# Second layer of a gated cross-attention network: transposed weights of both query tiles side by side, one product of 224 columns per head pair

## The chip, the cores and the metric

The kernel runs on one NeuronCore of a Trainium2 chip. The metric is the device time of one execution in microseconds; the median of three runs of the kernel before is 2099.33 us (2097.63 to 2100.96). All data are fp32 unless a line says otherwise. The engines are called PE (TensorE, the matmuls), VectorE (DVE), ScalarE (ACT), GpSimd (POOL) and SyncE (SP, which issues the DMAs); each of them takes its instructions in the order in which the program writes them for it.

## The reference

Eight batch elements, each with 224 tokens of 512 features and a context of 750 tokens of 512 features, go through two layers. A layer is a gated cross-attention and then a gated feed-forward network (FFN), each on the layer-normed input, each added back with a gate tanh(g):

```python
x = x + jnp.tanh(g_xattn[0]) * _L0_xattn_ref(_layernorm(x), ctx, ctx, ...)   # 16 heads of 32
x = x + jnp.tanh(g_ffn[0])   * _L0_ffn_ref(_layernorm(x), ...)               # ternary weights, conv, silu
x = x + jnp.tanh(g_xattn[1]) * _L1_xattn_ref(_layernorm(x), ctx, mask, ...)  # 8 heads of 64, masked
x = x + jnp.tanh(g_ffn[1])   * _L1_ffn_ref(_layernorm(x), ...)               # FP4-quantized weights and inputs
```

The change lies in the second layer's attention, of which this is the core:

```python
attn = jnp.einsum('bhnd,bhmd->bhnm', q, k) * SCALE      # 8 heads, 224 queries, 750 keys
attn = jnp.where(mask[:, None, :, :], attn, -jnp.inf)
attn = jax.nn.softmax(attn, axis=-1)
out = jnp.einsum('bhnm,bhmd->bhnd', attn, v)
```

## The kernel before

The main loop runs over n = 0 to 15: n = 0 to 7 are the batch elements in the first layer's attention (`attention16`), n = 8 to 15 the same elements in the second layer's (`attention8`). The text calls n = 8 "element 8" and so on. The last FFN of all elements follows in a stage of its own.

In `attention8` the 224 queries are cut into NT = 2 tiles of TP = 112, the 750 keys into NKT = 6 pieces of CP = 125, the eight heads into KC = 4 pairs g. One element is eight slots; slot = 2g + i is head pair g and query tile i, so even slots have i = 0 and odd slots i = 1. A slot does this:

1. PE: scores of both heads (L757, four matmuls of 375 columns, the two heads on the upper and lower 64 rows of the array), into two PSUM tiles `ps_half` of two banks each. There are two such tiles in all.
2. PE: the product of the values with the weights of the slot before (L720): 6 pieces x 2 heads, 112 columns each, heads side by side in the array's columns, summed in the bank `ps_pa`.
3. VectorE: mask and row maximum of each head (L774), its negative (L786).
4. ScalarE: exp with the row sum, one per head (L795), into the SBUF tile `room`.
5. PE: six transposes for each head (L817), from `room` back into a `ps_half` tile; a head's transposes need its exp.
6. ScalarE: the copy of each head's transposed weights into `room` as `pT` (L822), from where the next slot's product reads them. The next slot's scores need the same PSUM tiles, so they need these copies.

`weights_room` gives `p` and `pT` one of three stretches of `room` in turn. When both tiles of two head pairs are through, `divided` splits the reciprocal row sums (L731, L458, L462), transposes them (L468, copied by ScalarE as `sT`, L470), spreads them over the rows (L738, copied as `inv`, L742) and multiplies the product bank by them (L746). The last product and the second `divided` of an element run inside the next element (`rest`).

The order of the work around this is written by a planner with nominal costs. Other work stands in queues of generators whose pieces carry nominal PE and VectorE microseconds: the values and keys of this and the next element (L383, L325, copied by ScalarE, L392 and L334), the queries (L200, L354; L201, L363), the output projection (L429, L440), and `beside`, which holds the last part of the first FFN (L961, L1040, L1075) and the FP4 quantization and transposition of the last FFN's weights (`fp4_steps` L1115 to L1130, transposes L1156, copies L1174 and L1184). `fill(us, queue)` takes pieces until `us` of nominal PE time are used; `pace(us, beside)` takes pieces until VectorE has `us` of nominal work since the maxima. `finish` empties a queue. A slot fills 0.8 and 1.0 ahead of the two exps, 1.2 ahead of the transposes and 1.7 behind them (3.0 in the last element); `finish(values)` in slot 1 makes sure that the values are there for the first product. One pace call (1.5) stands ahead of the exps, one (3.5) behind them. Whatever copy a piece needs is written into ScalarE's order at the same place.

PSUM beside that: two banks `ps_m`, one `ps_t`, one `ps_pa`.

Of the kernel before, what the change touches and what calls it, by code (L numbers as in the profile page):

```python
# [36 lines left out]
B, S, D = 8, 224, 512  # L37
M = 750
TP = 112
# [3 lines left out]
KC = D // 128  # L43
MH = M // 2
WIDE = 500
CP = 125
NKT = M // CP
# [19 lines left out]
class Net:  # L67
# [125 lines left out]
    def transposed(self, dst, src, i, bank="t"):  # L193

        nc = self.nc
        half = src.dtype == BF16
        pt = self.ps(bank, [128, KC, TP], BF16 if half else F32)
        ident = self.ident16 if half else self.ident
        for k in range(KC):
            nc.tensor.transpose(pt[:, k, :], src[:, k * 128 : (k + 1) * 128], ident[:TP, :TP])  # L200
        nc.scalar.copy(dst[:, :, i * TP : (i + 1) * TP], pt)  # L201
# [499 lines left out]
    def attention8(self, n, soon, values, queue, beside, ends):  # L701

        nc, pool, job = self.nc, self.att, self.jobs[n]
        kT, qT = job["kT"], job["qT"]
        rows = [slice(h * 64, (h + 1) * 64) for h in range(2)]
        masks = self.masks(job["raw"])  # L710
        total = pool.tile([TP, NT, 2, KC], F32, name="total")
        banks = {}

        def product(g, i, pT):
            if g % 2 == 0 and i == 0:
                banks["pa"] = self.ps("pa", [128, 2, S])
            for j in range(NKT):
                for h, r in enumerate(rows):
                    col = g * 128 + h * 64
                    nc.tensor.matmul(  # L720
                        banks["pa"][r, g % 2, i * TP : (i + 1) * TP],
                        lhsT=job["v"][j][:, col : col + 64],
                        rhs=pT[:, h, j * TP : (j + 1) * TP],
                        start=j == 0,
                        stop=j == NKT - 1,
                    )

        def divided(pair):

            inv = pool.tile([TP, NT, 2, 2], F32, name="invs", bufs=2)  # L730
            nc.vector.reciprocal(inv, total[:, :, :, 2 * pair : 2 * pair + 2])  # L731
            transposed = self.stat_rows(self.stat[1][pair], inv)
            yield 0, 1.3
            sT = transposed("m")
            yield 0.1, 0.3
            pi = self.ps("t", [128, 2, S])
            for k in range(2):
                nc.tensor.matmul(  # L738
                    pi[:, k, :], lhsT=self.spread_r[:, k, :], rhs=sT, start=True, stop=True
                )  # L740
            across = pool.tile([128, 2, S], F32, name="inv")
            nc.scalar.copy(across, pi)  # L742
            yield 0.4, 0.6
            if pair == 0:
                job["aT"] = pool.tile([128, KC, S], F32, name="aT")
            nc.vector.tensor_tensor(  # L746
                job["aT"][:, 2 * pair : 2 * pair + 2, :], banks["pa"], across, ALU.mult
            )
            yield 0, 0.6

        before = None
        for slot in range(KC * NT):
            g, i = divmod(slot, NT)
            sc = [self.ps("half", [TP, 2, 512]) for _ in rows]
            for c in range(2):
                for h, r in enumerate(rows):
                    nc.tensor.matmul(  # L757
                        sc[h][:, c, :MH],
                        lhsT=qT[r, g, i * TP : (i + 1) * TP],
                        rhs=kT[g][r, c * MH : (c + 1) * MH],  # L760
                        start=True,
                        stop=True,
                    )
            if slot == 0:
                next(ends, None)
            elif slot == 1:
                self.finish(values)
            if slot:
                product(*before)
            nms = []  # L770
            for h in range(2):
                src = sc[h][:, :, :MH]
                mx = self.small.tile([TP, 1], F32, name="mx")
                nc.vector.tensor_tensor_reduce(  # L774
                    out=src,
                    in0=src,
                    in1=masks[i],
                    scale=1.0,
                    scalar=-MASKED,
                    op0=ALU.add,  # L780
                    op1=ALU.max,
                    accum_out=mx,
                )

                nms.append(self.small.tile([TP, 1], F32, name="nm"))
                nc.vector.tensor_scalar(nms[h], mx, -1.0e38, -1.0, ALU.max, ALU.mult)  # L786
            self.behind = 0
            if slot == 4:
                next(first)
            if not soon and (n + 1 < 2 * B or slot < 3):  # L790
                self.pace(1.5, beside)
            p = self.weights_room(TP, M, 2)
            for h, us in enumerate((0.8, 1.0)):
                self.fill(us, queue)
                nc.scalar.activation(  # L795
                    p[:, h, :].rearrange("p (c k) -> p c k", c=2),
                    sc[h][:, :, :MH],
                    AF.Exp,
                    bias=nms[h],
                    accum_out=total[:, i, h, g : g + 1],  # L800
                )
            if not soon:
                self.pace(3.5 if n + 1 < 2 * B or slot < 2 else 2.5, beside)
            self.fill(1.2, queue)
            if slot == 3:
                first = divided(0)
                next(first)
            if slot == 4:
                next(first)
            if slot == 4:  # L810
                next(first)
            pT = self.weights_room(CP, NKT * TP, 2)
            for h in range(2):
                pt = self.ps("half", [CP, 2, 512])
                half = NKT // 2
                for j in range(NKT):
                    nc.tensor.transpose(  # L817
                        pt[:, j // half, j % half * TP : (j % half + 1) * TP],
                        p[:, h, j * CP : (j + 1) * CP],
                        self.ident[:TP, :TP],  # L820
                    )
                nc.scalar.copy(  # L822
                    pT[:, h, :].rearrange("p (c k) -> p c k", c=2), pt[:, :, : half * TP]
                )
            before = g, i, pT
            self.finish(soon)
            self.fill(1.7 if n < 2 * B - 1 else 3.0, queue)
        if n < 2 * B - 1:
            self.finish(queue)
        second = divided(1)  # L830
        next(second)

        def rest():
            product(*before)
            yield 1.3, 0
            yield next(second)
            yield next(second)
            yield next(second)

        return rest()  # L840


# [771 lines left out]
```

## Time and profile before

| | us |
|---|---|
| median of 3 runs | 2099.33 |
| the profiled execution | 2097.81 |
| its span | 2096.0 |
| second layer's stretch, 1049 to 1718 | 669.00, PE busy 663.07 |
| VectorE, ScalarE, GpSimd busy in that stretch | 433.39, 301.72, 60.60 |
| L720, the product: 1536 records there | 87.72 busy |
| L817, the transposes: 768 records there | 94.05 busy |

A timeline row gives the start in the span, the length, the engine, the line, what is written and read, and how many records are merged in it. An fp32 matmul leaves two records, its two passes, a transpose leaves one: the program issues 12 matmuls L720 in each of 64 products, and the trace has 1536 records. A row of PE ends later than the next begins, as matmuls are pipelined, so the cost of a run on PE is read from its start to the next run's start. "PEld" are weight loads, which mostly lie beside a running matmul. A bracket at the end of a row is the engine's idle time ahead of it and what ended it. In a row of stretches the first number after the stretch is its length, then come each engine's busy time, the granted clock, the DMA share and GB/s.

### The profile page before, as it was taken

The page shows a single profiled execution, that of the slowest core. Times are in us where ns is not written, and L with a number is a line of the kernel's source. Part 1 is how long each engine was busy: PE and PEld are TensorE (multiplying, and loading weights), DVE is VectorE, ACT ScalarE, POOL GpSimd, SP SyncE. Part 2 cuts the span into 40 slices and gives each one's busy share as a digit, 9 for nine tenths or more (in the row PEclk, how much of TensorE's full clock was granted, in tenths as well). Part 3 has the DMA queues.
Part 4 walks back from the last instruction along what each step waited for, and adds up shares of the span by engine and source line. Part 5 has one row for each costly group of instructions (what it writes and reads, how often), then busy time and mean ns, then how long its engine had stood idle before and what let it go on. Part 6 is the DMA issues. An engine that isn't in the chain of part 4 may idle for free.

```text
span 2096.0 us, 32230 instructions
## 1 busy us (share of the span) xinstructions
PE 2057.1 (98%) x12606; PEld 1200.5 (57%) x12606; DVE 1382.3 (66%) x3587; ACT 947.4 (45%) x1812; POOL 130.5 (6%) x147
## 2 busy tenths in 40 slices
PE   9999999999999999999999999999999999999999
PEld 5454644546455464554656666666666665566554
DVE  4856776576675766667657577877743577676665
ACT  2554747557374573746736345445444321111111
POOL 0000000000000000000000011111100011111111
PEclk9999999999999999999999999999999999999999
DMA  7400001010010200112021122222310020000000
GB/s 252 140 1 30 21 22 47 1 49 19 24 44 1 63 6 28 40 41 67 31 82 38 55 88 64 78 80 74 96 60 30 16 90 11 12 14 20 20 11 15
DMA packets 59056, 98.65 MB, mean 47 GB/s; under 512 B 3684, under 2 KB 30052, under 8 KB 58776
## 3 DMA queue, kind: packets, MB, share of 16 engines
q1 hardware_dynamic: 58904, 96.59, 14.4%
q8 instruction: 99, 1.62, 0.3%
q14 instruction: 53, 0.43, 0.1%
HBM read 73.98 MB, written 22.60 MB: 46 GB/s over the span
## 4 chain that ended last, share of the span: by engine, by line
PE 92%; DVE 4%; ACT 3%; issue 1%; DMA 0%; SPq 0%; ACTq 0%; DVEq 0%
PE ps_m L383 16%; PE ps_m L325 14%; PE ps_big L1222 11%; PE ps_m L1254 6%; PE ps_m L354 5%; PE ps_pair L543 5%; PE ps_half L757 4%; PE ps_m L429 4%; PE ps_pa L629 4%; PE ps_half L817 4%; PE ps_pa L720 4%; PE ps_pair L489 3%; PE ps_t L961 2%; PE ps_m L1222 2%; PE ps_pair L480 2%; ACT room L519 1%
## 5 line engine op out<-in xcount | busy, mean ns | idle before, releaser
L325 PE MATMUL ps_m<-cx,wk 128*128 128x375 f32 x1024 | 366.4, 488 | 1.2 <-DMA wk<-in_L_Wk 1.2
L554 DVE CUSTOM_DVE_ANT_0 room<-ps_pair,zero 112x250 f32<-112x250 f32 (+1 forms) x512 | 247.2, 543 | 118.1 <-PE ps_pair L543 116.9
L519 ACT ACTIVATE room<-room,val 112x750 f32<-112x750 f32 x256 | 233.0, 914 | 73.2 <-DVE val L566 73.1
L325 PEld LDWEIGHTS ps_m<-cx,wk 128*128 128x128 f32 x1024 | 180.1, 190 | 113.3 <-issue 33.9
L774 DVE CUSTOM_DVE_ANT_0 ps_half<-ps_half,mbias 112x750 f32<-112x750 f32 x128 | 121.1, 946 | 127.5 <-PE ps_half L757 127.4
L654 ACT ACTIVATE room<-ps_pair 125x896 f32<-125x896 f32 x192 | 165.1, 912 | 63.9 <-PE ps_pair L489 63.9
L383 PE MATMUL ps_m<-wv_later,cx 128*125 128x512 f32 x384 | 185.8, 611 | 0.0
L383 PE MATMUL ps_m<-wv,cx 128*125 128x512 f32 x384 | 180.0, 603 | 0.0
L795 ACT ACTIVATE room<-ps_half,nm 112x750 f32<-112x750 f32 x128 | 113.5, 891 | 80.1 <-DVE nm L786 77.2
L1254 PE MATMUL ps_m<-wd,hqT 128*128 128x512 f32 x308 | 136.6, 592 | 0.0
L429 PE MATMUL ps_m<-wo,aT 128*112 128x512 f32 x256 | 117.3, 597 | 0.0
L1233 ACT ACTIVATE gth<-ps_big 128x352 f32<-128x352 f32 x48 | 22.3, 465 | 207.1 <-PE ps_big L1222 198.4
L383 PEld LDWEIGHTS ps_m<-wv,cx 128*125 128x125 f32 x384 | 67.6, 187 | 82.8 <-issue 73.4
L989 DVE SCALAR_TENSOR_TENSOR y<-hp,cw,y 128x224 f32<-128x224 f32 x256 | 109.5, 448 | 6.5 <-ACT y L975 2.0
L1222 PE MATMUL ps_big<-wg,xqT 128*128 128x352 f32 x352 | 111.3, 459 | 0.0
L1222 PE MATMUL ps_big<-wu,xqT 128*128 128x352 f32 x352 | 111.3, 459 | 0.0
L354 PE MATMUL ps_m<-xnT,wq 128*128 128x224 f32 x512 | 110.5, 359 | 0.6 <-ACT xnT L201 0.6
L383 PEld LDWEIGHTS ps_m<-wv_later,cx 128*125 128x125 f32 x384 | 66.3, 189 | 77.3 <-issue 74.5
L543 PE MATMUL ps_pair<-kT,qT 32*112 32x500 f32 (+1 forms) x1024 | 109.6, 507 | 0.8 <-ACT kT L334 0.6
L822 ACT COPY room<-ps_half 125x672 f32<-125x672 f32 x128 | 88.0, 720 | 48.2 <-PE ps_half L817 47.8
L392 ACT COPY v<-ps_m 125x512 f32<-125x512 f32 x62 | 36.3, 585 | 149.4 <-PE ps_m L383 149.1
L817 PEld LDWEIGHTS ps_half<-ident,room 112*125 112x125 f32 x768 | 93.4, 189 | 15.3 <-issue 7.8
(226 smaller groups left out, 3162.3 us busy)
## 6 DMA issues: line engine op xcount, KB each, us to landing
cx<-in_ctx SPq DMA_DIRECT2D x32, 750.0 KB
v_later<-vsome SPq DMA_DIRECT2D x34, 250.0 KB
v<-v_later SPq DMA_DIRECT2D x34, 250.0 KB
wst<-in_w SPq DMA_DIRECT2D x16, 512.0 KB
x<-in_x SPq DMA_DIRECT2D x8, 448.0 KB
mid<-x SPq DMA_DIRECT2D x8, 448.0 KB
x<-mid SPq DMA_DIRECT2D x8, 448.0 KB
last<-x SPq DMA_DIRECT2D x8, 448.0 KB
```

What stands on the lines that cost most here:

```text
L325: nc.tensor.matmul(pk, lhsT=self.w["wk"][:, k, g * 128 : (g + 1) * 128], rhs=job["cx"][c][:, k, :], start=k == 0, stop=k == KC - 1,)
L354: nc.tensor.matmul(pq[:, g - g0, :], lhsT=self.w["wq"][:, k, g * 128 : (g + 1) * 128], rhs=xnT[:, k, :], start=k == 0, stop=k == KC - 1,)
L383: self.nc.tensor.matmul(pv, lhsT=self.jobs[n]["cx"][c][:, k, at : at + CP], rhs=self.w[weight][:, k, :], start=k == 0, stop=k == KC - 1,)
L429: nc.tensor.matmul(po, lhsT=aT[:, g, i * TP : (i + 1) * TP], rhs=self.w["wo"][:, g, :], start=g == 0, stop=g == KC - 1,)
L519: nc.scalar.activation(whole[i][:, h, :], whole[i][:, h, :], AF.Exp, bias=val[:, i, g, h : h + 1], accum_out=sums[:, i, g, h : h + 1],)
L543: nc.tensor.matmul(sc[h // 2][:, h % 2, e * width : (e + 1) * width], lhsT=qT[r, g, i * TP : (i + 1) * TP], rhs=kT[g][r, k0:k1], start=Tru ...
L554: nc.vector.tensor_tensor_reduce(out=whole[i][:, h, k0:k1], in0=sc[h // 2][:, h % 2, e * width : (e + 1) * width], in1=self.zero[:TP].to_b ...
L654: nc.scalar.activation(p[:, 2 * k : 2 * k + 2, :], pw[k][:, :, : 2 * S], AF.Exp)
L774: nc.vector.tensor_tensor_reduce(out=src, in0=src, in1=masks[i], scale=1.0, scalar=-MASKED, op0=ALU.add, op1=ALU.max, accum_out=mx,)
L817: nc.tensor.transpose(pt[:, j // half, j % half * TP : (j % half + 1) * TP], p[:, h, j * CP : (j + 1) * CP], self.ident[:TP, :TP],)
L1222: nc.tensor.matmul(ps[:, :CW], lhsT=xqT[:, k, :], rhs=wt[:, k, c0 : c0 + CW], start=k == 0, stop=k == KC - 1,)
L1254: nc.tensor.matmul(po, lhsT=hqT[:, k, :], rhs=wd[:, k, :], start=k == 0, stop=k == NC1 - 1)
```

## The change

The transposed weights of both query tiles of a head pair now lie side by side: `pT` has one fixed place in `room`, shaped (head, key piece, 224 queries), and the copy of slot i writes its 112 columns of each key piece. `p` gets two fixed places behind it, one for each i. The product runs once for each head pair, in the even slots (and, for the last pair, in `rest`), as 12 matmuls of 224 columns. `finish(values)` moves from slot 1 to slot 2. The nominal filling becomes 0.4, 0.5 and 0.8 in even slots and 1.3, 1.5 and 1.5 in odd ones. Line numbers below are those of the kernel before; scores, exps, transposes and copies are the same in number and size.

```diff
-        def product(g, i, pT):
-            if g % 2 == 0 and i == 0:
+        def product(g):
+            if g % 2 == 0:
                 banks["pa"] = self.ps("pa", [128, 2, S])
             for j in range(NKT):
                 for h, r in enumerate(rows):
                     col = g * 128 + h * 64
                     nc.tensor.matmul(
-                        banks["pa"][r, g % 2, i * TP : (i + 1) * TP],
+                        banks["pa"][r, g % 2, :],
                         lhsT=job["v"][j][:, col : col + 64],
-                        rhs=pT[:, h, j * TP : (j + 1) * TP],
+                        rhs=pT[:, h, j, :],
...
-        before = None
+        pT = self.room[:CP, : 2 * NKT * S].rearrange("p (h j q) -> p h j q", h=2, j=NKT)
...
-            elif slot == 1:
+            elif slot == 2:
                 self.finish(values)
-            if slot:
-                product(*before)
+            if slot and i == 0:
+                product(g - 1)
...
-            p = self.weights_room(TP, M, 2)
-            for h, us in enumerate((0.8, 1.0)):
+            at = 2 * NKT * S + i * 2 * M
+            p = self.room[:TP, at : at + 2 * M].rearrange("p (h k) -> p h k", h=2)
+            for h, us in enumerate((1.3, 1.5) if i else (0.4, 0.5)):
                 self.fill(us, queue)
...
-            self.fill(1.2, queue)
+            self.fill(1.5 if i else 0.8, queue)
...
-            pT = self.weights_room(CP, NKT * TP, 2)
...
                 nc.scalar.copy(
-                    pT[:, h, :].rearrange("p (c k) -> p c k", c=2), pt[:, :, : half * TP]
+                    pT[:, h, :, i * TP : (i + 1) * TP].rearrange("p (c k) q -> p c k q", c=2),
+                    pt[:, :, : half * TP].rearrange("p c (k q) -> p c k q", k=half),
                 )
-            before = g, i, pT
...
         def rest():
-            product(*before)
-            yield 1.3, 0
+            product(KC - 1)
+            yield 2.6, 0
```

## The prediction

> **What bounds the kernel now.** I read the busy row first, then the chain that ended last, then the stretches of the second layer, then its timeline.
>
> ```profile
> PE 2057.1 (98%) x12606; PEld 1200.5 (57%) x12606; DVE 1382.3 (66%) x3587; ACT 947.4 (45%) x1812; POOL 130.5 (6%) x147
> ...
> PE 92%; DVE 4%; ACT 3%; issue 1%; DMA 0%; SPq 0%; ACTq 0%; DVEq 0%
> ```
>
> ```profile
> core 0: us, PE busy (x) PEld busy (x) DVE busy (x) ACT busy (x) POOL busy (x), PEclk, DMA share, GB/s
> 1220.10:1298.90 78.80, 78.80 (x529) 52.49 (x528) 59.87 (x143) 38.01 (x74) 10.95 (x11) 1.00 0.24 74
> ```
>
> TensorE (PE) is the bound: batch element 10 of the second layer takes 78.80 us and PE has work in every bit of them, at a granted clock of 1.00. So two things move the time: PE work saved, and any wait that PE now meets. The second is read from one even slot, slot 2 of element 11:
>
> ```profile
> 1321.37 1.37 PE L720 MATMUL ps_pa<-room,v 125*64 125x112 f32 x24
> ...
> 1322.67 0.66 PE L1156 MATMUL ps_t<-ident,wq 128*128 128x128 f32 x4
> ...
> 1323.16 2.74 PE L429 MATMUL ps_m<-wo,aT 128*112 128x512 f32 x6
> 1323.36 0.59 ACT L1174 COPY wg<-ps_t 128x512 f32<-128x512 f32 x1 [4.28 <-PE ps_t L1156]
> ...
> 1323.85 0.89 ACT L795 ACTIVATE room<-ps_half,nm 112x750 f32<-112x750 f32 x1
> ...
> 1324.72 0.89 ACT L795 ACTIVATE room<-ps_half,nm 112x750 f32<-112x750 f32 x1
> ...
> 1325.74 1.46 PE L817 MATMUL ps_half<-ident,room 112*125 112x112 f32 x12
> ```
>
> The reader is to see a hidden chain: product (L720), then four transposes of the last layer's FFN weights (L1156), then ScalarE's copy of these (L1174), and only behind that copy, in ScalarE's order, the two heads' exps (L795), for which PE's transposes (L817) wait. Counted from the product's start, the second exp ends at +4.24 and the second head's transposes start at +5.02 (4.37 and half of the run's 1.30): 0.78 us of slack, no more. That a late exp stops PE, and how soon after it PE goes on, shows once already, in slot 0 of element 8, on the row of weight loads: the exp ended at 1055.23, the load began at 1055.37, 0.14 later.
>
> ```profile
> 1055.37 1.37 PEld L817 LDWEIGHTS ps_half<-ident,room 112*125 112x125 f32 x8 [0.38 <-ACT room L795]
> ```
>
> **The product.** It takes 1.30 us now (1321.37 to 1322.67): 24 records, two passes for each of 12 matmuls, the two heads of a pair side by side, so 12 steps of about 0.096 us and some 0.15 of entry and exit. What a step takes at 224 columns stands in the first layer:
>
> ```profile
> 651.25 0.96 PE L629 MATMUL ps_pa<-room,v 125*32 125x224 f32 x16
> 652.14 1.02 PE L354 MATMUL ps_m<-xnT,wq 128*128 128x224 f32 x4
> ...
> 657.36 2.07 PE L354 MATMUL ps_m<-xnT,wq 128*128 128x224 f32 x10
> 659.26 2.69 PE L325 MATMUL ps_m<-cx,wk 128*128 128x375 f32 x8
> ```
>
> Ten passes of 224 columns take 1.90 us, 0.190 each; the first layer's own product, four heads side by side, takes 0.89 for four steps, 0.19 each and 0.13 around them. So a step costs its columns (112/224 of 0.190 is 0.095), and only the surroundings are saved. The new product is 12 x 0.19 + 0.10 = 2.38 us (the entry's 0.05 comes from a second weight load longer than a 112-column pass; a 224-column pass covers it). Two old products were 2.60: 0.22 saved per head pair, 32 pairs: **7.0 us**. Bounds: 0.15 of surroundings as now gives 2.43, 5.4 us; none at all gives 2.28, 10 us. I take 7.0, by the row nearest in shape.
>
> The Trainium skill, page "TensorE: Matmul & The Clock Gate", section "Back-to-back issue gap", gives sustained spacings of 81 ns per matmul at 128 columns and 131 at 512. By an estimate on the line between them 224 columns would cost only 1.18 times 112, the new product 1.54 us, and the saving would be 34 us. The rows above have twice the time for twice the columns, so the measurement decides.
>
> **The wait that it adds.** The work is the same elsewhere, but in even slots the product now stands 1.08 us longer (2.38 less 1.30) ahead of L1156, and so of L1174 and both exps, while the shares of filling work ahead of L817 are cut (0.4, 0.5 and 0.8 nominal us for 0.8, 1.0 and 1.2), so that L817 comes hardly later. Behind the exps in ScalarE's order wait its copies of the transposes; on PE everything waits behind L817. In the built program the filling in elements 10 to 13 is the same in each, so one element is enough. All times count from the product's start. Two passes of 512 columns are 0.86 us, of 375 are 0.64; L1156 is 0.49 (1322.67 to 1323.16); PE resumes 0.14 after an exp's end, plus 0.09 for a weight load no longer covered.
>
> - Slots 0 and 2: second exp ends at 4.24 + 1.08 = 5.32, release at 5.46. Slot 2: 2.38 + 0.49 + four L429 passes 1.72 puts L817 at 4.59 and its second head at 5.24: stall 0.22 + 0.09 = 0.3. Slot 0 has two passes of L468 (0.1) more: 0.2.
> - Slot 6: 2.38 + 0.49 + two L325 passes 0.64 + four L200 0.38 = 3.89, second head 4.54: stall 0.92 + 0.09 = 1.0.
> - Slot 4 has the copies sT (L470) ahead of the exps and kT (L334) between them:
>
> ```profile
> 1339.58 1.37 PE L720 MATMUL ps_pa<-room,v 125*64 125x112 f32 x24
> ...
> 1341.19 0.35 ACT L470 COPY sT<-ps_m 128x224 bf16<-128x224 bf16 x1 [3.71 <-PE ps_m L468]
> ...
> 1343.36 0.91 ACT L795 ACTIVATE room<-ps_half,nm 112x750 f32<-112x750 f32 x1
> ```
>
>  Its second exp ends at 4.69; 1.08 later is 5.77, and some 0.1 more because VectorE, which in the new order does the next element's norm statistics in slot 3 too (maxima 2.4, quantization 4.4, L440 0.7, statistics 1.8, the reciprocals' split 2.0, L188 0.5: 11.8 us of work by its rows, in a slot of 9.4), starts the maxima 2.3 late. PE arrives at 2.38 + 0.1 + 0.49 + 1.27 + 0.2 = 4.44, second head 5.09: stall 0.94 + 0.09 = 1.0. The same lateness holds the weights' transposes of slot 5 for 0.2.
> - Odd slots have no product ahead: L1156 0.49 and 3.4 to 4.3 us of filling, so exps end at about 2.4 and 3.5 and L817 starts at 3.8 to 4.7. No stall, and the product's 1.30 is simply gone.
>
> Sum 0.2 + 0.3 + 1.0 + 0.2 + 1.0 = 2.7 us an element, four elements: **+10.8 us**. Bounds: 0 (if the exps did not stand behind L1174) and 17 (every even slot held like slot 4).
>
> **The other four elements** (8, 9, 14, 15) are filled differently. Slot 0 of element 8: four passes of L429 instead of eight (1.7 us for 3.4) ahead of L817, whose exps are late because VectorE still finishes the first layer's quantization. PE arrives at 1053.9 and goes on at 1055.4, and stops 0.5 again for the second exp: stall about 2.0; but the 1.9 us for which PE waited there for xq (slot 2) goes, since these transposes come later behind the new product. Slot 4 of element 8 loses a filler between L961 and L738, which share one PSUM bank: 1.0. Slot 0 of element 15 has sT's copy between the exps, behind a product 1.08 longer: 0.9. Some others (0.8 at L1075, 0.4 at L200) vanish, some appear (0.4 each). Net +2.5, between -2 and +6. Nothing in PSUM, DMA or POOL is costed: on SP's queue the loads of the next values (L409) wait for the last product of the element before, 1.08 longer, with the FFN weights' loads (L1148) queued behind them, but the values are now needed in slot 2 instead of 1, some 9 us later, and the weights a slot after their load; DMA has a share of 0.24 there; ScalarE's copy (L822) writes as many elements, now in rows of 112 with a stride; the two of a slot end 1.0 us ahead of the next scores (1328.0 against 1329.04), which covers them up to 0.4 each; were each twice its 0.72, 0.4 a slot would show, 26 us in 64, and I take nothing, since no row here has an access pattern change a copy's time (L201's 448 elements, written in strided rows of 112, take 0.53, L742's 448 in one piece 0.54).
>
> **Sum.** -7.0 + 10.8 + 2.5 = +6.3 us on the profiled execution's 2097.81 (span 2096.0), so 2104.1. The median of the runs, 2099.33, stands 1.5 above that execution: **2105.6 us**, slower by 0.3%.
>
> **Rivals.**
> 1. About even (within 0.2%, the least that a measurement of this kernel can tell from no change): stalls of slots 4 and 6 half as long, because VectorE or the fillers fall differently than worked out; 10.8 becomes 6 to 7, net +1 to +2, 2101. For it: half of the stall rests on two slots; against: ScalarE's order is fixed in the program.
> 2. Not slower: the stalls do not come. It needs L1174 to be off the exps' path; then -7.0 and the others' +2.5 or less, 2092 to 2095. It decides where the stalls stay under 4.5 us in all, 0.3 a slot. The 0.78 us of slack against 1.08 speak against it.
> 3. No saving on PE: the wider product takes two old ones, 2.60. Then even slots are held 1.30 later instead of 1.08, +0.2 in 16 slots: 10.8 + 3.5 + 2.5 = 16.8, 2116. L354's and L629's 0.19 a step speak against it.
>
> **How the numbers follow.** Forecast 0.62, rival 1 0.22, rival 2 0.08, rival 3 0.08. The range goes from rival 1's lower side (stalls of 8 in all, 7.0 saved and the others at -2: 2098) to the bounds of 5.4 saved, 12.5 of stalls and +5 (2112). Slower by over 0.2%: forecast and rival 3, 0.70; same 0.22; faster 0.08.
>
> **What would show it.** L720: 768 records in 32 runs of about 2.4 us. PE idle before L817, ended by ScalarE's exps, in slots 4 and 6 of elements 10 to 13, about 1 us each and 10 in all, where there is none now; elements 10 to 13 at about 80.6 us instead of 78.8. Wrong if L817 shows no such waits, or if a 224-column step is not near 0.19.

## The result, and the profile after

The changed kernel takes 2111.32 us (median of four runs, 2107.62 to 2113.51), the kernel before 2099.32 (four runs as well): a ratio of 1.0055 (95% interval 1.0038 to 1.0073), slower by 0.55%. The forecast was 2105.6, slower by 0.3%, within 2098 to 2112. So the direction was right, and nearly twice as much time came on top as was worked out (12.0 us for 6.3). Below it is shown which terms of the sum held and which was missing.

In the changed kernel the exps stand in line 796, one below their place in the kernel before; the other lines named here have kept their numbers. The page's busy row and its chain, after:

```profile
PE 2063.1 (98%) x11838; PEld 1182.0 (56%) x11838; DVE 1377.0 (65%) x3587; ACT 947.9 (45%) x1812; POOL 130.2 (6%) x147
...
PE 89%; DVE 5%; ACT 4%; issue 1%; DMA 1%; POOL 0%; SPq 0%; ACTq 0%; POOLq 0%; DVEq 0%
```

768 matmul records fewer on PE, as they should be, and yet PE's share of the chain is smaller: 89% of the span for 92%, and VectorE, ScalarE and the DMAs each have one per cent more. Where it happens is read from the stretches of the program, cut at the first scores of each element and at the first L1222 of the last FFN's own stage:

```profile
core 0: us, PE busy (x) PEld busy (x) DVE busy (x) ACT busy (x) POOL busy (x), PEclk, DMA share, GB/s
0.00:1051.83 1051.83, 1022.66 (x7034) 546.96 (x7034) 696.67 (x2088) 596.75 (x1123) 16.11 (x34) 1.00 0.15 46
1051.83:1134.18 82.35, 79.68 (x466) 51.50 (x465) 54.39 (x136) 39.52 (x79) 3.02 (x4) 1.00 0.17 52
1134.18:1220.61 86.43, 84.84 (x455) 52.63 (x454) 56.77 (x138) 38.78 (x77) 4.46 (x5) 1.00 0.21 66
1220.61:1300.89 80.28, 79.31 (x433) 50.02 (x432) 58.39 (x139) 38.38 (x74) 10.93 (x11) 1.00 0.23 73
...
1541.39:1618.57 77.18, 76.19 (x409) 47.51 (x408) 25.83 (x75) 35.23 (x68) 2.33 (x3) 1.00 0.11 36
1618.57:1718.50 99.93, 98.15 (x481) 57.90 (x481) 52.16 (x130) 35.16 (x68) 5.86 (x7) 1.00 0.07 24
1718.50:2110.52 392.02, 384.67 (x1275) 225.67 (x1273) 260.73 (x467) 49.21 (x101) 55.55 (x50) 0.99 0.07 26
```

The reader is to see that element 10 now has 0.97 us without work on PE (80.28 less 79.31), where it had none, and that the last stage has 7.35, where it had 3.88. Beside the same stretches of the kernel before:

| stretch, us | before | after | difference |
|---|---|---|---|
| first layer | 1049.80 | 1051.83 | +2.0 |
| element 8 | 83.04 | 82.35 | -0.7 |
| element 9 | 87.24 | 86.43 | -0.8 |
| elements 10 to 13, together | 314.99 | 320.78 | +5.8 |
| element 14 | 77.96 | 77.18 | -0.8 |
| element 15 | 97.86 | 99.93 | +2.1 |
| second layer, sum of elements 8 to 15 | 661.09 | 666.67 | +5.6 |
| last FFN's stage | 385.14 | 392.02 | +6.9 |
| span | 2096.03 | 2110.52 | +14.5 |

The profiled execution after is 1 us above its median, that of before 1.5 below; the medians are 12.0 apart. The forecast was about the second layer, +6.3, and there it is +5.6. The last stage, in which the change edits nothing, costs more than all that.

Slot 2 of element 11, the slot that the prediction was worked out on, in the timeline after (start, length, engine, line):

```profile
1320.54 2.49 PE L720 MATMUL ps_pa<-room,v 125*64 125x224 f32 x24
...
1322.96 0.66 PE L1156 MATMUL ps_t<-ident,wq 128*128 128x128 f32 x4
...
1323.45 1.88 PE L429 MATMUL ps_m<-wo,aT 128*112 128x512 f32 x4
1323.66 0.58 ACT L1174 COPY wg<-ps_t 128x512 f32<-128x512 f32 x1 [5.40 <-PE ps_t L1156]
...
1324.14 0.89 ACT L796 ACTIVATE room<-ps_half,nm 112x750 f32<-112x750 f32 x1
...
1325.01 0.89 ACT L796 ACTIVATE room<-ps_half,nm 112x750 f32<-112x750 f32 x1
...
1325.17 1.59 PEld L817 LDWEIGHTS ps_half<-ident,room 112*125 112x125 f32 x12 [0.68 <-ACT room L796]
```

The product takes 2.42 us, from its start to that of L1156. The exps still stand behind L1174, and the first transposes L817 begin 0.14 after the first exp's end (1325.03). That idle time of the weight loads, ended by ScalarE, is the wait that the change brought. It is longest in slot 4, where both heads wait:

```profile
1344.24 0.91 PE L817 MATMUL ps_half<-ident,room 112*125 112x112 f32 x6
...
1345.48 0.91 PE L817 MATMUL ps_half<-ident,room 112*125 112x112 f32 x6 [0.33 <-ACT room L796]
```

The six transposes of the first head take 0.65 us where nothing waits (slot 2 of the kernel before); here the second head starts 1.24 behind the first. In the list of PE's waits over the whole second layer this wait is the first (us in all, times, the longest; the list leaves out what is hidden under the modelled ends of the matmuls), and in that of the kernel before L817 does not appear:

```profile
PE ps_half L817 <- ACT room L796: 6.7, 16, 1.2
```

And the last stage, first after and then before, from its timeline:

```profile
1734.08 2.63 PE L1222 MATMUL ps_big<-wg,wq 128*128 128x352 f32 x8 [0.34 <-DVE gth L1234]
1739.83 0.90 PE L1249 MATMUL ps_th<-ident,wq 128*128 128x128 f32 x3 [3.11 <-POOL wq L1130]
1740.53 4.90 PE L1222 MATMUL ps_big<-wu,wq 128*128 128x352 f32 x8
```

```profile
1728.34 0.49 PE L1249 MATMUL ps_th<-ident,wq 128*128 128x128 f32 x3
1728.66 2.53 PE L1222 MATMUL ps_big<-wu,wq 128*128 128x352 f32 x8
```

L1249 transposes the quantized hidden values of this stage's first tile. The quantization (L1115 to L1130) goes in pieces of 512 columns, each with VectorE work and one GpSimd multiplication (L1130), and is begun beside the second layer; the loop that ends the second layer stops once no piece is half done. Before, two of the three pieces were through by then, now it is one. The stage has to do one more on VectorE, PE waits 3.11 us for the last of them, and right behind that wait eight records L1222 (four matmuls) take 4.90 us instead of 2.53. The stretches there give the clock:

```profile
1739.50:1743.00 3.50, 3.17 (x8) 2.15 (x9) 3.36 (x5) 0.83 (x2) 0.28 (x1) 0.50 0.02 5
1743.00:1746.40 3.40, 3.40 (x8) 1.76 (x7) 3.29 (x6) 0.00 (x0) 1.39 (x1) 0.59 0.00 0
```

From the start of this L1249 to that of the second L1254 behind it PE takes 6.11 us, and 3.12 in the kernel before: the clock of about one half costs 3.0. The other 3.9 of the 6.9 have come by the time L1249 starts, 0.5 ahead of L1222 and the rest up to the end of the wait.

The first layer is the same program in both. In this execution it has a half clock at 356 to 360 us (0.57 granted there, 1.00 in the same place of before); half of those 3.4 us, 1.7, is an estimate of what that costs of its +2.0.

### The profile page after: what moved, and what is told of

The parts are those of the page before. It is cut to its first block, busy times and chain, and to the rows that moved or that the text cites. A ratio compares the mean times of both kernels' runs of the same rounds, so it can differ in the third digit from the quotient of the medians.

```text
span 2110.5 us, 30735 instructions
## 1 busy us (share of the span) xinstructions
PE 2063.1 (98%) x11838; PEld 1182.0 (56%) x11838; DVE 1377.0 (65%) x3587; ACT 947.9 (45%) x1812; POOL 130.2 (6%) x147
## 4 chain that ended last, share of the span: by engine, by line
PE 89%; DVE 5%; ACT 4%; issue 1%; DMA 1%; POOL 0%; SPq 0%; ACTq 0%; POOLq 0%; DVEq 0%
PE ps_m L383 16%; PE ps_m L325 13%; PE ps_big L1222 10%; PE ps_m L1254 6%; PE ps_m L354 5%; PE ps_pair L543 5%; PE ps_half L757 4%; PE ps_half L817 4%; PE ps_pa L629 4%; PE ps_m L429 4%; PE ps_pa L720 4%; PE ps_pair L489 3%; PE ps_t L961 2%; PE ps_m L1222 2%; PE ps_pair L480 2%; DVE hs L1061 1%
## 5 line engine op out<-in xcount | busy, mean ns | idle before, releaser
L1254 PE MATMUL ps_m<-wd,hqT 128*128 128x512 f32 x308 | 136.9, 593 | 0.0
L334 ACT COPY kT<-ps_m 128x375 f32<-128x375 f32 x128 | 60.2, 471 | 114.7 <-PE ps_m L325 113.7
L1222 PE MATMUL ps_big<-wu,xqT 128*128 128x352 f32 x352 | 111.3, 459 | 0.0
L1222 PE MATMUL ps_big<-wg,xqT 128*128 128x352 f32 x352 | 111.3, 459 | 0.0
L817 PEld LDWEIGHTS ps_half<-ident,room 112*125 112x125 f32 x768 | 93.5, 188 | 27.6 <-ACT room L796 17.6
```

Source lines behind the costliest of these rows:

```text
L817: nc.tensor.transpose(pt[:, j // half, j % half * TP : (j % half + 1) * TP], p[:, h, j * CP : (j + 1) * CP], self.ident[:TP, :TP],)
L1222: nc.tensor.matmul(ps[:, :CW], lhsT=xqT[:, k, :], rhs=wt[:, k, c0 : c0 + CW], start=k == 0, stop=k == KC - 1,)
L1254: nc.tensor.matmul(po, lhsT=hqT[:, k, :], rhs=wd[:, k, :], start=k == 0, stop=k == NC1 - 1)
```

## The experiments

Two theories stood against each other for the second layer. One: the wider product itself makes the wait, since the exps' chain (product, L1156, L1174, exps) is longer by what the product has grown, 1.12 us (2.42 less 1.30). The other: the filling between L1156 and L817 was cut (0.8 for 1.2 ahead of the transposes, 0.4 and 0.5 for 0.8 and 1.0 ahead of the exps), and PE would not wait if it had something to do there. For the last stage, theory and test were the number of pieces done ahead. All ratios are against the kernel before, run beside.

**e1: the product behind the pace call**, so that L1156 and L1174 stand ahead of it.

```diff
-            if slot and i == 0:
-                product(g - 1)
             nms = []
...
             if not soon and (n + 1 < 2 * B or slot < 3):
                 self.pace(1.5, beside)
+            if slot and i == 0:
+                product(g - 1)
```

> The changed kernel, with one edit: in even slots the product (L720) is written behind the four weight transposes L1156 instead of ahead of them, so their copy and both exps no longer stand behind it. Nothing else changes its place in elements 10 to 13. Theory (the longer product holds the copy and the exps, and PE stops at L817): the late second heads of L817 in slots 0, 2, 4 and 6 (0.15, 0.26, 0.85 and 0.96 us an element, read from the changed kernel's trace) go, and elements 10 to 13 fall from 80.28 to about 78.1 us each; the whole from 2111 to about 2102. Rival (the elements are longer because of the wider matmuls, or the copies in rows with a stride): they stay at 80.3 and the time at 2111.

Measured: 2107.51 us, ratio 1.0040 (1.0028 to 1.0052); elements 10 to 13 at 79.96, 79.95, 79.97 and 79.67. The waits for the exps in the second layer fell from 6.7 to 2.7 us, but the elements by 0.3 only, since a new wait came. PE's waits over elements 10 to 13 have one row, and the timeline of one slot 4 shows it:

```profile
PE ps_m L468 <- DVE stat L458: 4.3, 4, 1.2
```

```profile
1336.27 0.54 DVE L188 TENSOR_SCALAR xn<-x,mv,rstd 112x512 f32<-112x512 f32 x1
...
1336.42 0.27 PE L468 MATMUL ps_m<-ident,stat 112*128 112x112 bf16 x2 [1.05 <-DVE stat L458]
...
1336.72 0.94 DVE L772 CUSTOM_DVE_ANT_0 ps_half<-ps_half,mbias 112x750 f32<-112x750 f32 x1
```

In slot 4 the matmuls L468, which transpose the split reciprocals, now stand right behind the scores, while VectorE, late from slot 3, still works on the reciprocals (L458) and the next element's xn (L188); its maxima (L772 in this kernel) begin at 1336.72 only. The product used to cover that. So the first wait is tied to what stands behind the product, and the product had covered another. The expected 78.1 us an element did not come.

**e2: the filling ahead of the transposes turned round**, 1.7 nominal in even slots and 0.6 in odd ones.

```diff
-            self.fill(1.5 if i else 0.8, queue)
+            self.fill(0.6 if i else 1.7, queue)
```

> The changed kernel, with the filling ahead of L817 shared out anew: 1.7 instead of 0.8 nominal us in even slots, 0.6 instead of 1.5 in odd ones, the sum the same. The exps stay where they are. Theory: 0.9 us more of work covers the even slots' wait and the odd slots' L817, which has 1.1 to 2.3 us of slack, bears the loss: elements 10 to 13 at 78 to 78.5 us instead of 80.28, the whole at about 2103. Rival (wider matmuls or copies cost the time): 80.3 and 2111, as the amount of work is the same.

Measured: 2107.06 us, ratio 1.0035 (1.0022 to 1.0048); elements 10 to 13 at 79.81, 79.36, 79.80 and 79.24. In the even slots of elements 10 and 11 the second head's transposes now start 0.5 us or more after their exp's end, where 0.14 is what a wait leaves. But L817's waits are still 6.4 us in the second layer: they have moved into the odd slots (1 and 3), whose transposes come too soon with 0.6. The theory held for even slots, and the expected 78 to 78.5 us were missed, because the odd ones had been stripped.

**e3 and e4: one piece and two.** To the kernel before, a limit that leaves it with one quantized piece ahead:

```diff
             if f == 0:
-                beside.append(quantized(h["h"][f]))
+                beside.append(islice(quantized(h["h"][f]), 3))
```

and to the kernel after, a loop that goes on until two are through:

```diff
-        while beside and self.head["ready"] is None:
+        while beside and (self.head["ready"] is None or self.head["ready"] < 2 * D):
             self.piece([beside])
```

> The kernel before, in which only the first of the three pieces of the first hidden tile (L1115 to L1130) is quantized ahead of the last FFN, as came about in the changed kernel, instead of two. Attention is left as it was. Theory (the changed kernel's last stage is 6.9 us longer because one piece more of 512 columns is left to VectorE and GpSimd there, for which PE stops 3.1 us at L1249 and then runs at half clock for 6.8 us): before becomes 5 to 7 us slower, 2104 to 2106, with the wait at L1249 in its trace. Rival (the last stage is longer because of the clock alone, which fell there by chance): 2099, no wait.

> The changed kernel, in which a second piece of the first hidden tile is quantized ahead of the last FFN, as in the kernel before. Theory: the last stage falls from 392 to about 385 us, the wait at L1249 goes, and the whole is 5 to 7 us faster than the changed kernel, 2104 to 2106. Rival (clock by chance): 2111, with the stage at 392 or the half clock elsewhere.

Measured: the kernel before with one piece 2103.51 us (1.0025, 1.0014 to 1.0035), last stage 390.67 for 385.14; the kernel after with two pieces 2104.69 (1.0028, 1.0017 to 1.0040), last stage 385.14, elements 10 to 13 as before this edit (80.31 three times, 79.93). The waits of e3's last stage begin with the same row as those of the kernel after:

```profile
PE ps_th L1249 <- POOL wq L1130: 3.1, 1, 3.1
```

So the last stage's cost can be put in and taken out with one piece: +5.5 on the stage of before, -6.9 on that of after (2111.32 to 2104.69 in the medians). Up to L1249 both are 3.9 to 4.0 late; the difference is the half clock, which costs 1.5 in e3 and 3.0 in the kernel after. e3's median rose by 3.8 only, less than the 5 to 7 expected; its twelve runs spread from 2101.5 to 2111.4, and its profiled execution has no half clock in the first layer, where that of before has one. The cost is an effect of where the change's filling left the pieces, and no part of the attention. What was left, 1.0028, is the second layer's.

**e5: exps first.** The edits of e5, e6, e7 and e10 stand on e4. In elements 10 to 15 the first pace call only in odd slots, so that in even slots L1156 and L1174 come behind both exps; the filling is the same piece for piece.

```diff
-            if not soon and (n + 1 < 2 * B or slot < 3):
+            if (i or n < B + 2) and not soon and (n + 1 < 2 * B or slot < 3):
                 self.pace(1.5, beside)
```

> The kernel with two quantization pieces done ahead (e4_two_pieces), and in elements 10 to 15 the first pace call only in odd slots, so that in even slots the transposes L1156 and their copy L1174 stand behind the two exps; the filling ahead of the transposes is the same, piece for piece. Theory (the exps are late because they stand behind L1174, and L1174 behind the product): the waits of slots 0, 2 and 6 go (0.15, 0.26 and 0.96 of lateness), slot 4 keeps about 0.9, since there the copies of sT and kT stand ahead of the exps and VectorE's maxima begin 1.3 late. Elements 10 to 13 fall from 80.3 to 78.9, the median by 4 times 1.4 from 2104.7 to about 2099. Rival (PE waits for something else, the PSUM bank or the strided copy): elements stay at 80.3, the median at 2104.7.

In this order one matmul of the last FFN's first tile (L1222) stands ahead of the transposes L1211 that write its input, so that tile is computed from other data; the instructions are the same in number and size. Measured: 2108.53 us, ratio 1.0048 (1.0035 to 1.0060), 4 us more than e4. Element 10 takes 81.02 for 80.31 (elements 11 and 13 have a half clock in addition). The lateness in slot 2 went as expected (the second exp is done 1.75 us ahead of its transposes) and in slot 6 it fell from 0.96 to some 0.6; in slot 0 it rose from 0.15 to 0.4, as sT's copy L470 now stands between the exps. But slot 4 of every one of elements 10 to 13 got a worse wait, here that of element 11:

```profile
1345.14 0.59 ACT L1174 COPY wu<-ps_t 128x512 f32<-128x512 f32 x1
1345.78 0.35 PE L738 MATMUL ps_t<-sT,spread 128*128 128x224 bf16 x2 [1.71 <-ACT wu L1174]
```

L738 writes the one bank `ps_t`, in which L1156's result still lies until L1174 has copied it, and L1174 now comes last. The theory had left the bank out; the rival named a PSUM bank, but for times that stay as they are. So both miss: the exps' chain is what it was said to be, and moving L1174 out of it is no cure.

**e6: the filling balanced**, 1.7 nominal ahead of the transposes in even slots, 0.9 in odd ones.

```diff
-            self.fill(1.5 if i else 0.8, queue)
+            self.fill(0.9 if i else 1.7, queue)
```

> e4_two_pieces with a nominal filling ahead of the transposes of 1.7 in even slots and 0.9 in odd ones (for 0.8 and 1.5). The order written shows one more piece (L383, L429 or two of L325) ahead of L817 in each even slot of elements 10 to 13, and in the odd ones about as much work as before. Theory (a new wait because the filling between L1156 and L817 was cut while the exps' chain kept its length): no wait at L817 in elements 10 to 13, so 78.83 less 4 products of 0.18, 78.1 each, the median about 2096, between 2094 and 2099 as the other elements fall. Rival (a chain that waits whatever stands beside it, the waits only change place as in e2_fill_even): 79.4 to 79.8, median 2102.

Measured: **2089.91 us** (2088.94 to 2091.16), ratio 0.9953 (0.9941 to 0.9966): faster than both kernels, by 0.47% against the one before. Its stretches for elements 10 and 11, and the last row of PE's waits over its whole second layer:

```profile
1213.37:1291.76 78.39, 78.34 (x433) 49.77 (x433) 56.79 (x137) 38.08 (x74) 10.48 (x10) 1.00 0.25 74
1291.76:1369.35 77.59, 77.59 (x429) 49.30 (x428) 55.99 (x134) 38.04 (x73) 10.82 (x11) 1.00 0.24 72
```

```profile
PE ps_half L817 <- ACT room L796: 0.2, 1, 0.2
```

PE has work in all of element 11. Elements 10 to 13 average 77.94, 0.81 less than before, where the shorter product accounts for 0.72. In twelve of their sixteen even slots the exps are about as late as in the changed kernel (the second one ends 5.3 to 5.8 us after the product's start), and PE is busy until then; in the other four the moved filling has put L1174 behind both exps, and they end at 3.6 or 4.7. So a late exp costs nothing where PE has enough to do ahead of the transposes. The other gain is in element 8 (79.03 for 83.04) and 9 (84.89 for 87.24); it was not foreseen, and with it the median is 4 us below the 2094 to 2099 expected.

**e7: the wide product cut in two**, 112 columns for each query tile, one straight after the other, in the same place. Two loops around the same matmul:

```diff
-            for j in range(NKT):
+            for i in range(NT):
+                for j in range(NKT):
...
-                        banks["pa"][r, g % 2, :],
+                            banks["pa"][r, g % 2, i * TP : (i + 1) * TP],
...
-                        rhs=pT[:, h, j, :],
+                            rhs=pT[:, h, j, i * TP : (i + 1) * TP],
```

> e4_two_pieces with the wide product cut into two of 112 columns, one for each query tile, one right after the other in the same place. All else stands as it is. Theory: the run L720 takes 2.60 in place of 2.42, and since the exps' chain and the work ahead of L817 both stand behind it, the waits stay as they are: elements 10 to 13 from 80.3 to 81.0, the median by 32 times 0.18 to 2110.5. Rival (a longer product by itself adds to every wait, as the prediction's third case has it): 0.18 more in each of three waits an element too, 81.5, median 2113. If 224 columns save nothing: 80.3 and 2104.7.

Measured: 2104.93 us, ratio 1.0029 (1.0019 to 1.0039), the same as e4; elements 10 to 13 at 80.41, 0.1 more. Slot 2 of element 11 in its timeline (lines one further down in this kernel):

```profile
1322.08 2.52 PE L721 MATMUL ps_pa<-room,v 125*64 125x112 f32 x48
1324.53 0.66 PE L1157 MATMUL ps_t<-ident,wq 128*128 128x128 f32 x4
```

Forty-eight passes of 112 columns take 2.45 us, twenty-four of 224 take 2.42. I had expected 2.60, twice the old product. So of the 0.18 saved by a head pair 0.15 is for standing together, one entry and one exit of a run less, and only 0.03 for being wide. What came out in time is the last case of the expectation, that 224 columns save nothing against two runs of 112 in a row. The waits stayed as they are, as the theory has it (over the second layer those for the exps sum to 6.8 us here and to 6.9 in e4), but with a product only 0.03 longer this says little about what a longer product does.

**e8: the filling alone**, on the kernel before; its product stays in every slot with 112 columns.

```diff
-            for h, us in enumerate((0.8, 1.0)):
+            for h, us in enumerate((1.3, 1.5) if i else (0.4, 0.5)):
...
-            self.fill(1.2, queue)
+            self.fill(1.5 if i else 0.8, queue)
```

> The kernel before with the changed filling alone (0.4, 0.5 and 0.8 in even slots, 1.3, 1.5 and 1.5 in odd ones); the product stays as it is, once in each slot, 112 columns. Theory (the cut of the filling makes the wait, the longer product only moves both sides): exps end 4.24 behind the product's start as before, in slot 4 4.69, and PE comes to the second head's transposes at 4.26, 3.94, 3.76 and 3.72 in slots 0, 2, 4 and 6: lateness 0.2, 0.5, 1.2 and 0.75, elements 10 to 13 81.4 in place of 78.83, the median 2110 or more. Rival (the longer product makes the wait): 78.8 to 79.2, median 2100 to 2102.

Here three matmuls L1222 stand ahead of L1211, and the last FFN's first tile is computed from other data, with the same instructions. Measured: 2124.89 us, ratio 1.0124 (1.0108 to 1.0139); elements 10 to 12 at 81.77, 81.76 and 81.76, the last stage 390.57 with its wait of 3.1. Slot 2 of element 11:

```profile
1330.76 1.37 PE L720 MATMUL ps_pa<-room,v 125*64 125x112 f32 x24
...
1334.11 0.89 ACT L795 ACTIVATE room<-ps_half,nm 112x750 f32<-112x750 f32 x1
...
1334.28 1.60 PEld L817 LDWEIGHTS ps_half<-ident,room 112*125 112x125 f32 x12 [0.67 <-ACT room L795]
```

The product is the old one, its second exp ends where it ended before (4.24 after the product's start), and the transposes wait all the same, because PE comes too soon. Counted from record to record, against the spacing that the same two lines have where nothing waits, L817 is 2.3 us late in an element (1.2 ahead of its runs, 1.1 inside them, where the second head waits), not far from the 2.65 worked out. Counted in the same way the changed kernel has 2.4: the cut filling makes nearly the whole of that wait without the wide product. The rest of the 2.9 us that an element grew, 0.7, lies in slot 5 ahead of L200, the transposes of the next queries, which the odd slots' larger filling now brings sooner; 0.5 of it is a wait for VectorE's xn (L188):

```profile
1360.75 2.69 PE L325 MATMUL ps_m<-cx,wk 128*128 128x375 f32 x8
1363.94 0.57 PE L200 MATMUL ps_m<-ident,xn 112*128 112x112 f32 x4 [0.50 <-DVE xn L188]
```

The changed filling alone is worse than the whole change; element 8 (88.97 for 83.03, 1.7 of it a half clock) and the last stage add to it.

**e9 and e10: two controls of e6.** e9 gives the old product e6's filling (and the old one in the last element) and the two pieces of e4, e10 gives e6 the old filling in the last element, by the same condition on n.

```diff
-            for h, us in enumerate((0.8, 1.0)):
+            for h, us in enumerate((0.8, 1.0) if n + 1 == 2 * B else (1.3, 1.5) if i else (0.4, 0.5)):
...
-            self.fill(1.2, queue)
+            self.fill(1.2 if n + 1 == 2 * B else 0.9 if i else 1.7, queue)
```

> The kernel before, its product as it was (once in each slot, 112 columns), with the filling of e6_fill_17_09 (0.4, 0.5 and 1.7 in even slots, 1.3, 1.5 and 0.9 in odd ones; the last element keeps 0.8, 1.0 and 1.2) and two quantization pieces done ahead. Theory 1 (what e6_fill_17_09 gained beyond the product's 5.8 us comes from the filling in elements 8 and 9, where PE no longer waits): elements 10 to 13 without a wait at L817, 78.8 each, elements 8 and 9 together some 3 to 5 us shorter than before, the median 2095 to 2096.5. Theory 2 (the gain in elements 8 and 9 needs the moved product): elements 8 and 9 within 1 us of before, the median 2098 to 2100.

> e6_fill_17_09 with the old filling (0.8, 1.0 and 1.2) in the last element alone, where L1222 waited 1.6 for VectorE's L1234 and the element took 99.0 for 97.87 before. Theory (that wait comes from where the filling of slot 4 leaves the pieces of the first tile's gate): the wait falls below 0.5, element 15 at 97.5 to 98, the median 2088.5 to 2089.5. Rival (the wait stands with the wide product in that element): 99.0 and 2089.9. A gain of 1 us is near what the runs can tell; the element's length and the wait decide.

Measured: e9 2111.65 us, ratio 1.0058 (1.0044 to 1.0072); element 8 takes 86.78 and 9 takes 88.30, longer than before by 3.7 (1.7 of it a half clock) and 1.1, and elements 10 to 13 take 80.2 to 81.2. Its product still stands in odd slots, where this filling adds 1.0 nominal us ahead of the exps; L200 waits 7.5 us in the second layer, 2.3 before. Both theories of it miss on the bad side. e10: 2089.94, ratio 0.9950 (0.9937 to 0.9963), no different from e6; the last element takes 99.51 for 99.00, and the wait of L1222 for L1234 in it stays at 1.6, so it does not come from that filling, as the rival has it; what it does come from is open. This last element is also the one place where the wide product stands with the old filling: in its even slots the second exps end 0.4 to 1.6 us ahead of their transposes, and none waits. Between e9 and e10 lies only the edit of the product, with its place, that of `finish(values)` and the fixed places in `room`, 22 us with the same filling: what e6 gained beyond the product's 5.8 it owes to neither part alone.

## Why the prediction was right in direction, and short by half

- **The product.** Predicted 2.38 us and 7.0 saved; measured 2.42 and 5.8 (64 runs of 1.302 against 32 of 2.422, from a run's start to the next one's), inside the bounds of 5.4 and 10. The failing piece is the 0.05 of the entry, which the wider pass was to cover; it was not covered (the first step of a run takes 0.24 us, the others 0.19). That a step costs its columns held (0.19 for 0.096), and e7 shows the reason given to be right in kind: the surroundings are saved, the columns cost the same. The prediction had set its rows above its estimate of 34 us saved from the Trainium skill ("TensorE: Matmul & The Clock Gate", section "Back-to-back issue gap"), and the measured 5.8 agrees with the rows.
- **The wait in even slots, elements 10 to 13.** Predicted 2.7 us an element, 10.8 in all. The four elements grew by 5.8 while their 16 products saved 2.9, so 8.7 came, 2.2 an element. By slot of element 11, from the second head's start: 0.15 in slot 0 (0.2 predicted), 0.22 in slot 2 (0.3), 0.85 in slot 4 (1.0), 0.96 in slot 6 (1.0), nothing in slot 5 (0.2). The release 0.14 after an exp, and the second exp's end (5.36 after the product's start in slot 2, 5.32 predicted) came out to a few hundredths. Mis-sized were the 0.09 for an uncovered weight load, of which next to nothing shows, and VectorE's lateness in slot 4: its maxima began 1.2 late, not 2.3.
- **What makes this wait.** The prediction named both, the longer product and the cut filling, and put the weight on the first ("1.08 us longer ahead of L1156"). e6 and e8 put it on the second: no wait with the long product and enough filling, nearly the same wait (2.3 us an element for 2.4) with the short product and the cut filling. The product stands ahead of the transposes as well as of the exps, so its 1.1 us move both sides, and the 0.78 of slack against 1.08 was no measure of a wait. The lengths added up either way, which is why the number came out.
- **The other four elements.** Predicted net +2.5; they shortened by 0.2 in all while 16 products saved 2.9, so +2.7. The wait for xq in element 8 (1.9) went, as said; slot 4 there waits 0.7 (1.0 predicted).
- **The step that failed: the sum ends with the second layer.** The prediction let "the change" cost nothing after element 15, while it moved the `beside` pieces all along. The last stage's 6.9 us (wait and half clock, e3 and e4) is more than the second layer's 5.6. That the time still lies within 2098 to 2112 is luck: the upper end was made of dearer stalls, a smaller saving and dearer other elements, none of which came so dear, and the room left for them took in a term that was not in the sum. Without it (e4) the time is 2104.7, where 2105.6 was forecast. The trace of before held the warning: its first tile's last transposes L1249 come without a wait, with two pieces done ahead; in the order that the changed program gives VectorE the second piece stands behind the last L746 and L440, where it had stood ahead of them.
- **Rivals.** About even (stalls half as long) would have held for the second layer with stalls of 6 to 7; they were 8.7. "The stalls do not come" needed L1174 to be off the exps' path; e5 took it off, and L738 waited in its stead. e6 shows that it was not needed: there no even slot of elements 10 to 13 waits, and in twelve of these sixteen L1174 still stands ahead of the exps. "No saving on PE" is refuted by 2.42 against 2.60.
- The first layer's +2.0 is mostly a half clock of this one execution: the wait of 1.3 us ahead of it, at L480, stands in all twelve kernels and has a half clock behind it in three profiles (after, e2, e4).

## What to carry to other kernels

Where work is merged into fewer, longer runs, the fillers around it can matter more than the merging: try several fillings on both layouts and look, slot by slot, at when each side of the next wait is ready (here 1.7 and 0.9 instead of 0.8 and 1.5 turned 0.3% lost into 0.5% gained). Follow moved background work to its end, past the edited part: a piece that is left over costs where nothing stands beside it. And before merging, ask what is saved: here two runs put together saved 0.15 us, and wider matmuls 0.03.

## What was not expected of the hardware

- After a short wait PE may go on at a granted clock of one half for 3.4 us, or twice that. In all five kernels with the 3.1 us wait for L1130 (after, e1, e2, e3, e8) a half clock shows at that place and the last stage takes 390.4 to 392.0; in the seven without the wait (before, e4, e5, e6, e7, e9, e10) there is none, and the stage takes 385.13 or 385.14. The Trainium skill ("TensorE: Matmul & The Clock Gate", section "HAM oscillation — how this bites in real kernels") warns of idle gaps above some 3.4 us; here a half clock came behind shorter ones, so the measurement decides. In e5, two of four waits of 1.7 us were followed by one (granted clock 0.57 over 1347 to 1351), two were not; an element then takes 82.7 in place of 81.0. So a wait on PE can cost some 1.7 us more than its length, and 3.0 where the half clock lasts twice as long; what decides whether it comes is not shown.
- Twice as many passes of half the columns cost the same (2.45 against 2.42 us). What costs some 0.15 is the run: its first step is 0.05 longer than the others, of 112 columns as of 224, and some 0.10 lies behind its last one. What these two are is not shown.
